# Two graph-attention layers: a block's leftovers held behind a step, and moved weight tiles summed in SBUF

## The chip, the cores and the metric

One NeuronCore of a Trainium2 chip runs the whole program. The metric is the device time of one execution in microseconds (us). Engines are named as in the profile: PE is TensorE (PEld its weight loads), DVE is VectorE, ACT is ScalarE, POOL is GpSimd, SP is SyncE, which here only issues transfers.

## The reference

4096 nodes with 512 features and a 4096 x 4096 adjacency `adj` pass through two layers. All data are float32. Cut to what matters:

```python
# layer 0, h = relu(layernorm(x)); 4 heads of 128
sig = sigmoid(f1[:, :, None] + f2[:, None, :])
att = softmax(where(adj != 0, adj * sig, -inf))     # both patterns are adj
Xa  = einsum('hij,hjd->hid', att, Xw)               # encoder attention
emb = mlp_block(batchnorm(Xa))
Y   = einsum('hij,hjd->hid', att, emb)              # decoder attention, the same att
out = mlp_block(elu(Y @ W.T));  x = x + out
# layer 1, h = relu(layernorm(x)); 4 heads of 128
logits = leaky_relu(e_s[:, :, None] + e_n[:, None, :]) - 1e10 * (1 - adj)
x = x + relu(einsum('hnm,hmo->hno', softmax(logits), feats) + b)
```

So there are three attentions: encoder, decoder (it uses the encoder's weights and denominators again) and the last one, in the second layer.

## The kernel before

Features lie on the partitions, nodes along the free dimension. One function, `attention`, is used three times. It works in 8 blocks, one for each head h and each half tb of the target nodes (TB = 2048). A block walks over NJ = 32 steps j of 128 source nodes. In a step

- SP loads a 256 KB mask tile `a` (5 buffers);
- the weights of 128 sources by 2048 targets are made in a 1 MB tile `e`: in encoder and decoder by Tanh (L402) and Exp (L403) on ACT and the multiplication by the mask on DVE (L404); in the last attention by one ACT operation (L771) and one on DVE (L772);
- PE multiplies the tile into four PSUM banks `po` (L334; the fourth bank is opened in step EVICT = 2, and catches up with L331).

The tiles `e` come from a ring: two buffers in a pool that lives through layer 0 and `ebufs` in the attention's own pool, so 9 in the encoder and in the last attention, and 6 in the decoder. A tile that nobody has finished with holds up ACT's first operation nine steps later.

The softmax's denominator is a sum over all sources. Each step's tile goes into it in one of three ways, which a table of steps lays down (`ENC_FIRST` for the encoder's first two blocks, `ENC` for its others, `GAT` for the last attention):

- *by ones*: PE multiplies the tile by a column of ones into the bank `den` (L288);
- *added*: DVE adds the tile to an SBUF tile `acc` (L352, L354; in the last attention it is a part of R[2]);
- *moved*: a GpSimd-issued DMA adds the tile to the DRAM tile `dacc[tb]` (L346; a block's first move is a plain copy). In step NJ - 2 the sum is loaded back into a tile of the ring (L304).

At the end of a block PE multiplies the loaded sum and `acc` by ones as well. `ENC_FIRST` has no moved steps and 12 by ones; `ENC` has 9 moved and 6 by ones; `GAT` has 11 moved and 3 by ones.

What remains of a block, its *leftovers*, is done in the course of the next block. The function `at(j, f)` files it under a step, and the loop calls it at the beginning of that step: in step 2 the denominators are copied out (L235 on ACT) and sent through DRAM into a column (L236 and L238 on GpSimd's queue), and the four banks are evicted (L496 on DVE in the encoder, L607 or L776 on ACT in the others); in step 7 the column is inverted (L242, L243) and stored as a row (L244); in steps 8, 9, 14 and 15 each of four pieces of that row is broadcast to a tile `rb` (L249, 2 buffers); in steps 13, 14, 19 and 20 the results are scaled by it (L500, or L780 in the last attention), and one step later they are finished (L503 statistics in the encoder; L613 to L615 in the decoder; L783 and an addition to the output in DRAM, L789, in the last attention). The decoder has no L242, as it takes the encoder's rows.

In the encoder every fifth tile is also stored in DRAM for the decoder (L321, L372 on ACT's queue).

The order in which a step's instructions are traced is not the order of an engine's queue. A scheduler that knows only modelled durations lays out each engine's queue ahead of time: of the instructions that it takes to be ready, it issues the one traced first. An instruction whose operands it takes to be ready early can so come before work of earlier steps. `tc.issue_after(ins)` forbids this for one place: instructions traced inside it that run on the engine of `ins` come behind `ins` in that engine's queue, without a wait. On the chip each queue is worked off in order.

Of the kernel before, what the change touches and what calls it, by code (L numbers as in the profile page):

```python
# [20 lines left out]

# [1 line left out]

# [6 lines left out]
FP = mybir.dt.float32  # L32
U8 = mybir.dt.uint8
AF = mybir.ActivationFunctionType
ALU = mybir.AluOpType
# [4 lines left out]
N, F, H, D, P = 4096, 512, 4, 128, 128  # L40
IB = 512
NIB = N // IB
NJ = N // P
C = IB // P

TB = 2048
NTB = N // TB
SB = TB // IB
# [8 lines left out]
TINY = 1e-30  # L57
# [4 lines left out]
ENC_FIRST = (), (4, 5, 10, 11, 15, 16, 20, 21, 25, 26, 30, 31)  # L62
ENC = (0, 3, 6, 9, 12, 15, 18, 21, 24), (4, 5, 13, 14, 30, 31)
GAT = (0, 2, 5, 7, 10, 12, 15, 17, 20, 22, 25), (9, 30, 31)
# [15 lines left out]
def kernel(ctx, tc, x, xT, adjT, w0, w0T, v0, wencT, wdecT, vecs, w1, w1T, a1, outT):  # L80
    nc = tc.nc
    consts = ctx.enter_context(tc.tile_pool(name="consts", bufs=1))
    dram = ctx.enter_context(tc.tile_pool(name="dram", bufs=1, space=DRAM))
# [5 lines left out]
    R = [big.tile([P, N], FP, name=f"R{i}") for i in range(5)]  # L89
# [30 lines left out]
    jcol = consts.tile([P, NTB, H, NJ // NTB], FP, name="jcol")  # L120
    jcol2 = consts.tile([P, NTB, H, NJ // NTB], FP, name="jcol2")
    nq = consts.tile([P, NTB, H, NJ // NTB], FP, name="nq")

    def column(t, j, h):
        j = j % (NJ // NTB), j // (NJ // NTB)
        return t[:, j[1], h, j[0]:j[0] + 1]
# [19 lines left out]
    ekeep = [[[dram.tile([P, TB], FP, name=f"ekeep{h}_{t}_{k}") for k in range(NJ // KEEP)] for t in range(NTB)]  # L146
             for h in range(H)]

    dacc = [dram.tile([P, TB], FP, name=f"dacc{n}") for n in range(2)]

    masks = [[dram.tile([MG * P, TB], U8, name=f"mask{t}_{g}") for g in range(NJ // MG)] for t in range(NTB)]

# [43 lines left out]
    def load_mask(a, tb, j):  # L196

        return nc.sync.dma_start(a, masks[tb][j // MG][(j % MG) * P:(j % MG + 1) * P, :])


    def attention(what, keep, pools, weights, values, row_of, out, finish, ebufs, modes=None, invert=None,
                  kept=None, sums=None, extras={}, row0=None, masks0=()):

# [15 lines left out]
        spool, made, masks0 = pools, 0, list(masks0)  # L221
        if invert is not None:
            acc = spool.tile([P, TB], FP, name="acc") if sums is None else sums

        def weight_tile():
            nonlocal made
# [45 lines left out]
            load_row(rowb, *row_of(h, tb))  # L272
            return rowb

        later, last_ones, last_main = {}, None, None
        rowb = row0 if row0 is not None else next_row_of(0, 0)
        blocks = [(h, tb) for h in range(H) for tb in range(NTB)]
        for n, (h, tb) in enumerate(blocks):
# [6 lines left out]
            def add_to_den(t, stop=False):  # L285
                nonlocal begun, last_ones
                for s in range(SB):
                    last_ones = nc.tensor.matmul(den[s * 32:(s + 1) * 32, :], ones[:, 0:32], t[:, s * IB:(s + 1) * IB],  # L288
                                                 start=not begun, stop=stop)
                begun = True  # L290
# [1 line left out]
            po, ahead = [bank() for _ in range(SB - 1)], []  # L292
            adds, held, back, stores, next_row = [], [], None, [], None
            for j in range(NJ):
                for f in later.pop(j, []):
                    f()
                with tc.issue_after(a_load.ins) if j else nullcontext():
                    if (n, j) in extras:
                        extras[n, j](a_load)
                    if not last and j == NJ - 10:  # L300
                        next_row = next_row_of(*blocks[n + 1])
                if moved and j == NJ - 2:
                    back = weight_tile()
                    nc.gpsimd.dma_start(back, dacc[tb])  # L304
                e = weight_tile()
                store = j % KEEP == KEEP - 1 and kept is not None
                if store and kept == "read":
                    a_load = nc.sync.dma_start(e, ekeep[h][tb][j // KEEP])
                else:
                    if masks0:  # L310
                        a, a_load = masks0.pop(0)
                    else:
                        a = mask_tile(keep)
                        a_load = load_mask(a, tb, j)
                    weights(e, rowb, a, j, h, SB if n + j == 0 else 1)
                    if store:
                        stores.append((j // KEEP, e))

                    if j % KEEP == KEEP - 3 and stores:
                        k, t = stores.pop()  # L320
                        nc.scalar.dma_start(ekeep[h][tb][k], t)  # L321

                def products():
                    nonlocal last_main, last_ones

                    with tc.issue_after(last_ones.ins) if last_ones is not None else nullcontext():

                        if j == EVICT:
                            po.append(bank())
                            for k, t in ahead:  # L330
                                nc.tensor.matmul(po[-1], block(values[h], k), t[:, (SB - 1) * IB:SB * IB],  # L331
                                                 start=(k == 0), stop=False)
                        for s, b in enumerate(po):
                            last_main = nc.tensor.matmul(b, block(values[h], j), e[:, s * IB:(s + 1) * IB],  # L334
                                                         start=(j == 0), stop=(j == NJ - 1))
                    last_ones = None


                early = last and j == NJ - 1 and invert is not None
                if not early:  # L340
                    products()
                if j < EVICT:
                    ahead.append((j, e))
                if invert is not None:
                    if j in moved:
                        nc.gpsimd.dma_start(dacc[tb], e, **({"accum_op": ALU.add} if j > moved[0] else {}))  # L346
                    elif j in by_ones:
                        held.append(e)
                    else:
                        adds.append(e)  # L350
                        if len(adds) == 2:
                            nc.vector.tensor_add(acc, *adds)  # L352
                        elif len(adds) > 2:
                            nc.vector.tensor_add(acc, acc, e)  # L354

                    if held and j + 1 not in by_ones:
                        with tc.issue_after(last_main.ins):
                            for t in held:
                                add_to_den(t)
                        held = []  # L360
                    if j == NJ - 1:
                        with tc.issue_after(last_ones.ins) if last_ones is not None else nullcontext():
                            if back is not None:
                                add_to_den(back)
                            add_to_den(acc, True)
                if early:
                    products()
# [32 lines left out]
    def tanh_weights(e, rowb, a, j, h, parts):  # L400
        for e, rowb, a in in_parts(parts, e, rowb, a):
            nc.scalar.activation(e, rowb, AF.Tanh, bias=column(score[:, 1], j, h), scale=0.5)  # L402
            nc.scalar.activation(e, e, AF.Exp, scale=0.5)  # L403
            nc.vector.tensor_mul(e, e, a)  # L404

    a_att, b_att, a_mlp, b_mlp = (coefs[:, k, :] for k in range(4))

    with tc.tile_pool(name="keep", bufs=1) as keep:
# [116 lines left out]
        with tc.tile_pool(name="enc", bufs=1) as spool:  # L525

            with tc.issue_after(last_act.ins), tc.issue_after(masks0[-1][1].ins):
                attention("enc", keep, spool, tanh_weights, R[0:4], lambda h, tb: (rows[tb], h), out_enc,
                          (scaled, statistics), 7, lambda n: ENC if n > 1 else ENC_FIRST, (TINY, ALU.max), "write",
                          row0=row0, masks0=masks0,  # L530
                          extras={(1, 12): lambda load: copy_adjacency(7, load),
                                  (2, 8): encoder_weights, (H * NTB - 1, NJ // 2): three_heads})
# [232 lines left out]
    def gat_weights(e, rowb, a, j, h, parts):  # L765
        for e, rowb, a in in_parts(parts, e, rowb, a):

            if parts > 1:
                nc.vector.tensor_scalar(rowb, rowb, mbc[:, h:h + 1], G_MAX, ALU.add, ALU.min)
                nc.scalar.activation(rowb, rowb, AF.Exp, scale=0.8)  # L770
            nc.scalar.activation(e, rowb, AF.Relu, bias=column(nq, j, h), scale=column(jcol, j, h))  # L771
            nc.vector.scalar_tensor_tensor(e, e, column(jcol2, j, h), a, ALU.add, ALU.mult)  # L772

    def out_gat(spool, h, tb, s, po):
        o = R[2][:, TB + s * IB:TB + (s + 1) * IB]
# [15 lines left out]
    with tc.tile_pool(name="gat", bufs=1) as spool:  # L791
        x1_last = []

        def load_last(load):
            x1_last.append(spool.tile([P, TB], FP, name="rowb", bufs=2))
            nc.sync.dma_start(x1_last[0], outT[(H - 1) * P:H * P, (NTB - 1) * TB:NTB * TB])

        attention("gat", spool, spool, gat_weights, v1, lambda h, tb: (rowsg, tb * H + h), out_gat,
                  (scaled_gat, add_to_output), 7, lambda n: GAT, (N * TINY, ALU.add), sums=R[2][:, 0:TB], row0=row0,
                  extras={(H * NTB - 1, NJ - 10): load_last})  # L800


# [40 lines left out]
```

## Time and profile before

| | us |
|---|---|
| median of 3 runs | 3362.6 (3361.0 to 3365.4) |
| the profiled execution: its own time | 3363.46 |
| its span, from first to last instruction | 3361.7 |
| encoder attention, first to last product | 69.7 to 1115.1 |
| decoder attention | 1261.3 to 2150.3 |
| last attention | 2414.8 to 3351.2 |
| PE busy | 3246.9 |
| DVE busy | 2680.3 |
| ACT busy | 2601.9 |

The mean granted TensorE clock was 0.987. In the profile, an instruction's line is followed by its operation and by out<-in in the program's names of tiles. "Idle before" is the time that the engine stood still just ahead of it, and "<-" names what ended that. The windows view gives the busy time of each engine in a stretch and the number of instructions begun there in brackets. A queue with a q behind the engine's name is that engine's sequencer, which issues transfers. One matmul of 512 float32 columns shows as two instructions, 0.43 us apart, so a step has 8 in the row L334; four products by ones run side by side in the array, so their rows overlap.

### The profile page before, as it was taken

To read this page: it belongs to the slowest core of one execution; us is meant where nothing else is said; L and a number is where in the kernel's file an instruction comes from. 1 tells how busy PE (TensorE), PEld (TensorE's weight loads), DVE (VectorE), ACT (ScalarE), POOL (GpSimd) and SP (SyncE) were. 2 spreads that over 40 slices of the span, in tenths; PEclk is the share of its full clock that TensorE was granted. 3 is DMA by queue.
4 is the path that set the end of the run, shared out by engine and by line. 5 is a ranking of instruction groups with operands and counts; after the bars stand their busy time and mean duration, and the time that the engine had idled before them with its cause. 6 is when DMAs were issued, how large, how long until landed. Compare 5 with 4: busy or idle time off the path is not lost. (4 is left out here: it accounts for less than half of the span.)

```text
span 3361.7 us, 26034 instructions
## 1 busy us (share of the span) xinstructions
PE 3246.9 (97%) x8943; PEld 1495.3 (44%) x8943; DVE 2680.3 (80%) x1912; ACT 2601.9 (77%) x1908; POOL 327.4 (10%) x479
## 2 busy tenths in 40 slices
PE   7999999999999999999999999999999999999999
PEld 6334334334334464444444444447644444443443
DVE  6999889889888775665666566486599999989999
ACT  7989999999999438999999999566655665665654
POOL 2000110110110000000000000024301111111111
PEclk9999999999999999999999999999999999999999
DMA  9985768768777103443443443232288898788877
GB/s 204 195 178 166 213 195 235 216 196 233 213 212 199 43 13 138 138 135 128 147 151 124 138 145 130 75 113 95 69 205 204 203 229 207 196 198 207 212 191 173
DMA packets 180309, 559.60 MB, mean 166 GB/s; under 512 B 20372, under 2 KB 23700, under 8 KB 144208
## 3 DMA queue, kind: packets, MB, share of 16 engines
q0 software_dynamic: 43232, 211.14, 31.8%
q1 hardware_dynamic: 126288, 293.66, 25.6%
q10 hardware_dynamic: 10656, 53.15, 4.0%
q8 instruction: 70, 1.15, 0.1%
q14 instruction: 63, 0.52, 0.0%
HBM read 391.78 MB, written 233.19 MB: 186 GB/s over the span
## 5 line engine op out<-in xcount | busy, mean ns | idle before, releaser
L334 PE MATMUL ps<-e,R 128*128 128x512 f32 x6048 | 2651.6, 598 | 77.4 <-DVE e L404 60.4
L334 PEld LDWEIGHTS ps<-e,R 128*128 128x128 f32 x6048 | 1149.2, 191 | 1570.6 <-issue 1420.9
L404 DVE TENSOR_TENSOR e<-e,a 128x2048 f32<-128x2048 f32 (+1 forms) x470 | 1050.6, 2260 | 385.6 <-ACT e L403 363.7
L402 ACT ACTIVATE e<-rowb,score 128x2048 f32<-128x2048 f32 (+1 forms) x470 | 913.3, 1968 | 85.0 <-PE ps L334 47.4
L403 ACT ACTIVATE e<-e 128x2048 f32<-128x2048 f32 (+1 forms) x470 | 872.3, 1881 | 29.9 <-DVE e L404 23.5
L771 ACT ACTIVATE e<-rowb,nq,jcol 128x2048 f32<-128x2048 f32 x224 | 457.9, 2087 | 208.6 <-DMA dacc<-e 132.3
L772 DVE SCALAR_TENSOR_TENSOR e<-e,jcol,a 128x2048 f32<-128x2048 f32 (+1 forms) x259 | 590.6, 2319 | 3.8 <-ACT e L771 3.8
L354 DVE TENSOR_TENSOR R<-R,e 128x2048 f32<-128x2048 f32 x128 | 292.0, 2282 | 0.0
L354 DVE TENSOR_TENSOR acc<-acc,e 128x2048 f32<-128x2048 f32 x126 | 288.3, 2288 | 2.3
L346 POOL DMA_DIRECT2D dacc<-e x142 | 118.5, 835 | 1213.8 <-DMA dacc<-e 413.7
L543 PE MATMUL ps<-R,w 128*128 128x512 f32 x512 | 220.3, 592 | 0.6 <-DVE w L510 0.6
L249 POOL DMA_DIRECT2D rb<-rinvs x88 | 52.8, 652 | 1118.6 <-DVE R L500 903.9
L543 PEld LDWEIGHTS ps<-R,w 128*128 128x128 f32 x512 | 97.2, 190 | 122.7 <-issue 118.2
L717 PE MATMUL ps<-w1x,hT 128*128 128x260 f32 x512 | 117.8, 389 | 2.8 <-ACT hT L693 2.8
L563 ACT ACTIVATE ex<-ps,bias 128x512 f32<-128x512 f32 x64 | 44.0, 687 | 97.2 <-PE ps L543 80.1
L783 ACT ACTIVATE R<-R,vec 128x512 f32<-128x512 f32 x32 | 23.0, 720 | 110.4 <-DVE R L780 110.1
L717 PEld LDWEIGHTS ps<-w1x,hT 128*128 128x128 f32 x512 | 97.9, 193 | 22.8 <-ACT hT L693 4.4
L500 DVE TENSOR_TENSOR R<-R,rb 128x512 f32<-128x512 f32 x60 | 40.5, 685 | 70.7 <-DMA rb<-rinvs 58.6
L288 PE MATMUL den<-e,ones 128*32 128x512 f32 x784 | 93.6, 598 | 0.0
L771 ACT ACTIVATE e<-w,nq,jcol 128x2048 f32<-128x2048 f32 (+1 forms) x35 | 65.6, 1939 | 32.9 <-DMA dacc<-e 30.2
L565 DVE SCALAR_TENSOR_TENSOR ex<-ex,re 128x512 f32<-128x512 f32 x64 | 45.0, 703 | 35.8 <-ACT re L564 35.7
L722 ACT ACTIVATE R<-ps,rstd 128x128 f32<-128x128 f32 x128 | 38.7, 367 | 40.2 <-PE ps L717 39.2
(154 smaller groups left out, 1217.0 us busy)
## 6 DMA issues: line engine op xcount, KB each, us to landing
a<-mask SPq DMA_DIRECT2D x720, 256.0 KB, 3.6
dacc<-e POOLq DMA_DIRECT2D x142, 1024.0 KB, 8.6
ekeep<-e ACTq DMA_DIRECT2D x48, 1024.0 KB, 5.7
e<-ekeep SPq DMA_DIRECT2D x48, 1024.0 KB, 4.8
rb<-rinvs POOLq DMA_DIRECT2D x88, 256.0 KB, 3.8
mask<-in_adjT POOLq DMA_DIRECT2D x8, 2048.0 KB, 76.6
rowb<-rows SPq DMA_DIRECT2D x16, 1024.0 KB, 5.2
e<-dacc POOLq DMA_DIRECT2D x14, 1024.0 KB, 5.1
```

The lines of the kernel that those rows point to most:

```text
L249: nc.gpsimd.dma_start(rb, everywhere(rinvs[h][tb], 0, s * IB, IB))
L288: last_ones = nc.tensor.matmul(den[s * 32:(s + 1) * 32, :], ones[:, 0:32], t[:, s * IB:(s + 1) * IB], start=not begun, stop=stop)
L334: last_main = nc.tensor.matmul(b, block(values[h], j), e[:, s * IB:(s + 1) * IB], start=(j == 0), stop=(j == NJ - 1))
L346: nc.gpsimd.dma_start(dacc[tb], e, **({"accum_op": ALU.add} if j > moved[0] else {}))
L354: nc.vector.tensor_add(acc, acc, e)
L402: nc.scalar.activation(e, rowb, AF.Tanh, bias=column(score[:, 1], j, h), scale=0.5)
L403: nc.scalar.activation(e, e, AF.Exp, scale=0.5)
L404: nc.vector.tensor_mul(e, e, a)
L543: nc.tensor.matmul(z, w[:, fb, o * P:(o + 1) * P], nodes(src[fb], ib), start=(fb == 0), stop=(fb == C - 1))
L717: nc.tensor.matmul(b[:, 0:2 * DX], hT[:, fb, c * P:(c + 1) * P], w1x[:, fb, 2 * k:2 * k + 2, :].rearrange("p h x -> p (h x)"), start=(fb = ...
L771: nc.scalar.activation(e, rowb, AF.Relu, bias=column(nq, j, h), scale=column(jcol, j, h))
L772: nc.vector.scalar_tensor_tensor(e, e, column(jcol2, j, h), a, ALU.add, ALU.mult)
```

## The change

Two things are changed together.

*Pins.* The functions that make weights now return their last ACT and their last DVE instruction. The leftovers filed under a step j are traced inside `pinned(products_of)`, that is, behind these two instructions of the last step whose weights were computed. Transfers that GpSimd or SP issue and PE's instructions are not held by it.

*The moved tiles' sum.* From an attention's second block on, moved tiles are added to a tile in SBUF, `sums2`, and PE takes it from there; nothing is loaded back. Only a first block with moved steps (the last attention's) still goes by DRAM, through one tile `dacc` in place of two. In the encoder the tile is new (`acc2`, 8 KB in each partition), and `ebufs` goes from 7 to 6, so that its ring has 8 tiles. In the last attention it is `row0`, the tile that held the first block's row (in memory, the decoder's weights `w`), and the ring stays at 9. There is one `sums2` for all blocks, where `dacc` had one tile for each half.

```diff
-    dacc = [dram.tile([P, TB], FP, name=f"dacc{n}") for n in range(2)]
+    dacc = dram.tile([P, TB], FP, name="dacc")
...
+    @contextmanager
+    def pinned(behind):
+
+        with ExitStack() as stack:
+            for i in behind:
+                stack.enter_context(tc.issue_after(i.ins))
+            yield
...
+            sums2 = spool.tile([P, TB], FP, name="acc2") if sums2 is None else sums2
...
-                for f in later.pop(j, []):
-                    f()
+
+                with pinned(products_of):
+                    for f in later.pop(j, []):
+                        f()
...
-                if moved and j == NJ - 2:
+                if n == 0 and moved and j == NJ - 2:
                     back = weight_tile()
-                    nc.gpsimd.dma_start(back, dacc[tb])
+                    nc.gpsimd.dma_start(back, dacc)
...
-                    weights(e, rowb, a, j, h, SB if n + j == 0 else 1)
+                    products_of = weights(e, rowb, a, j, h, SB if n + j == 0 else 1)
...
-                        nc.gpsimd.dma_start(dacc[tb], e, **({"accum_op": ALU.add} if j > moved[0] else {}))
+                        nc.gpsimd.dma_start(sums2 if n else dacc, e, **({"accum_op": ALU.add} if j > moved[0] else {}))
...
-                            if back is not None:
-                                add_to_den(back)
+                            if moved:
+                                add_to_den(sums2 if n else back)
                             add_to_den(acc, True)
...
-            nc.scalar.activation(e, e, AF.Exp, scale=0.5)
-            nc.vector.tensor_mul(e, e, a)
+            last_act = nc.scalar.activation(e, e, AF.Exp, scale=0.5)
+            last_dve = nc.vector.tensor_mul(e, e, a)
+        return last_act, last_dve
...
-                          (scaled, statistics), 7, lambda n: ENC if n > 1 else ENC_FIRST, (TINY, ALU.max), "write",
+                          (scaled, statistics), 6, lambda n: ENC if n > 1 else ENC_FIRST, (TINY, ALU.max), "write",
...
-            nc.scalar.activation(e, rowb, AF.Relu, bias=column(nq, j, h), scale=column(jcol, j, h))
-            nc.vector.scalar_tensor_tensor(e, e, column(jcol2, j, h), a, ALU.add, ALU.mult)
+            last_act = nc.scalar.activation(e, rowb, AF.Relu, bias=column(nq, j, h), scale=column(jcol, j, h))
+            last_dve = nc.vector.scalar_tensor_tensor(e, e, column(jcol2, j, h), a, ALU.add, ALU.mult)
+        return last_act, last_dve
...
-                  (scaled_gat, add_to_output), 7, lambda n: GAT, (N * TINY, ALU.add), sums=R[2][:, 0:TB], row0=row0,
+                  (scaled_gat, add_to_output), 7, lambda n: GAT, (N * TINY, ALU.add), sums=R[2][:, 0:TB],
+                  sums2=row0, row0=row0,
```

More of the change, by code (lines that the diff above doesn't have):

```diff
@@ L24 @@
-from contextlib import ExitStack, nullcontext
+from contextlib import ExitStack, contextmanager, nullcontext
 import concourse.bass as bass
@@ L198, in load_mask @@
         return nc.sync.dma_start(a, masks[tb][j // MG][(j % MG) * P:(j % MG + 1) * P, :])
+    @contextmanager
[4 more added lines that the diff above has]
+            yield
     def attention(what, keep, pools, weights, values, row_of, out, finish, ebufs, modes=None, invert=None,
-                  kept=None, sums=None, extras={}, row0=None, masks0=()):
+                  kept=None, sums=None, sums2=None, extras={}, row0=None, masks0=()):
         spool, made, masks0 = pools, 0, list(masks0)
@@ L273, in next_row_of @@
             return rowb
-        later, last_ones, last_main = {}, None, None
+        later, last_ones, last_main, products_of = {}, None, None, ()
         rowb = row0 if row0 is not None else next_row_of(0, 0)
```

## The prediction

> **What bounds the kernel now.** I read the page first, then busy time in windows cut at the blocks, then the waits, and then the order of one engine's queue at the start of a block. The page's first line says that TensorE is busy nearly all the time, so anything that shortens another engine counts only where TensorE waits for it:
>
> ```profile
> PE 3246.9 (97%) x8943; PEld 1495.3 (44%) x8943; DVE 2680.3 (80%) x1912; ACT 2601.9 (77%) x1908; POOL 327.4 (10%) x479
> ```
>
> A busy matmul row is no proof of full pace, so I cut the three attentions into their eight blocks each (from the first matmul of a block to the next one's):
>
> ```profile
> core 0: us, PE busy (x) PEld busy (x) DVE busy (x) ACT busy (x) POOL busy (x), PEclk, DMA share, GB/s
> ...
> 595.20:722.20 127.00, 120.25 (x324) 50.44 (x320) 114.78 (x63) 119.21 (x65) 11.89 (x17) 0.99 0.76 215
> ...
> 1381.10:1491.00 109.90, 109.90 (x258) 48.67 (x257) 65.98 (x39) 102.95 (x61) 2.15 (x4) 1.00 0.41 138
> ...
> 2762.50:2877.30 114.80, 114.80 (x301) 49.54 (x297) 110.38 (x55) 70.96 (x42) 16.40 (x22) 1.00 0.83 208
> 2877.30:2994.80 117.50, 115.77 (x300) 49.22 (x296) 111.80 (x56) 70.96 (x42) 17.21 (x23) 1.00 0.83 205
> 2994.80:3116.10 121.30, 116.52 (x300) 48.98 (x296) 112.50 (x56) 70.55 (x42) 17.25 (x23) 1.00 0.82 199
> ```
>
> Decoder blocks (1381 on) take 109.9 us with TensorE busy for 109.90: nothing is to be had there. The last attention's block 3 runs at 114.8, all TensorE; blocks 4 to 7 take 117.5, 121.3, 117.7 and 117.4. An encoder block (block 4, at 595) takes 127.0 with TensorE 120.25, ScalarE 119.21, VectorE 114.78: three engines near their limit and none full, the mark of engines stalling one another. The waits name the stalls:
>
> ```profile
> DVE R L500 <- DMA rb<-rinvs: 58.6, 19, 7.9
> ACT dsb L235 <- PE den L288: 45.4, 7, 11.2
> PE ps L334 <- DVE e L404: 60.4, 35, 5.2
> DVE dcol L242 <- DMA dcol<-dens: 30.8, 7, 8.8
> ```
>
> And the timeline of VectorE at the start of encoder block 4 shows where the first of them lies:
>
> ```profile
> 586.58 4.49 DVE L404 TENSOR_TENSOR e<-e,a 128x2048 f32<-128x2048 f32 x2
> ...
> 597.72 4.49 DVE L404 TENSOR_TENSOR e<-e,a 128x2048 f32<-128x2048 f32 x2 [4.25 <-ACT e L403]
> ...
> 605.10 4.49 DVE L404 TENSOR_TENSOR e<-e,a 128x2048 f32<-128x2048 f32 x2 [0.31 <-ACT e L403]
> 616.85 0.69 DVE L500 TENSOR_TENSOR R<-R,rb 128x512 f32<-128x512 f32 x1 [7.26 <-DMA rb<-rinvs]
> ```
>
> Count the masks' multiplications L404: steps 0 to 5, and then the scaling L500 of the block before, which the program traces in step 13. The scheduler has put it seven steps early, where its row of reciprocals has not landed, and all of VectorE stands behind it for 7.26 us. In the last attention the timelines of GpSimd and VectorE show the other one, at block 7:
>
> ```profile
> 3244.47 0.86 POOL L346 DMA_DIRECT2D dacc<-e  x1 [8.69 <-issue]
> 3245.03 0.86 POOL L236 DMA_DIRECT2D dens<-dsb  x1
> 3252.79 0.59 POOL L238 DMA_DIRECT2D dcol<-dens  x1 [6.89 <-DMA dens<-dsb]
> ...
> 3254.66 0.17 DVE L242 TENSOR_SCALAR dcol<-dcol 128x16 f32<-128x16 f32 x1 [5.66 <-DMA dcol<-dens]
> ```
>
> The denominators were in SBUF by 3235.9 (their copy is ScalarE's L235), but their 8 KB transfer stands in GpSimd's queue behind the third moved tile of the block, which waits for the landing of the second (3243.68), and then it lands with that tile.
>
> **The change, part by part.** (1) *Pins.* No instruction is added. Leftovers of a block on ScalarE and VectorE may no longer come before the weights of step j-1. I compared queue positions: eviction L496 and copy L235 already stand behind step 1 in the encoder, as traced in step 2, so the 45.4 us wait of L235 is not touched; in the last attention L776, L780 and L242 stand at or behind their traced steps too, so there the pins are void. In the decoder L500 and L613 to L615 move about ten steps later; about 10 of L500's 58.6 us lie there and cost nothing, since TensorE covers them (109.90 of 109.9); without that cover it would be those 10. What moves in the encoder is L242 (from behind step 3 to 6), L500 and L503 (from behind 5 to 7 to behind 12 to 20).
>
> The rb chain gets time: L242 behind step 6 runs near 615; rinvs behind a moved tile took 5.7 us in this block, so near 621 to 625; rb took 5.7 us, 631 to 635; step 12 ends on VectorE near 638. So the 7.3 us wait goes (48 us in the encoder). What is late next? From ScalarE's restart after L235 (595.9) its Exp rows L403 come in pairs every 7.39 us, so that of step 16 ends at 649.4. VectorE, no longer late, idles before step 16 and starts it at 649.4; before, it started it at 653.3. From there to the end of step 30's multiplication it was busy without a gap, 58.2 us (to 711.5); the second half of the leftovers, 4 rows of 0.6 to 0.7, now falls into this stretch: 60.7. Then 10.9 us to the end of the denominator on TensorE, as before. A block from restart to restart: 0.6 + 53.5 + 60.7 + 10.9 = 125.7. So of 7.3 us only about 1.4 come back: VectorE's own work in the second half (five additions in a row in steps 25 to 29) and ScalarE's wait for the denominator keep the rest. Against 130.4, 126.7, 127.1, 127.3, 126.9 for blocks 2 to 6 (between L235 rows) this is 4.7 + 1.0 + 1.4 + 1.6 + 1.2 = 9.9. Block 1 differs: from 260 on TensorE has no gap, and its 6 us of gaps (steps 3 to 10) come just from VectorE being late by the leftovers; later these meet a lead, so I take 5 of the 6. Block 7 gets 1.5 as its neighbours do; its wait for the bias product, 7.8 us at L517, isn't pinned and stays. Encoder: 16.4.
>
> (2) *Moved tiles into SBUF.* 142 moves before and after (6 x 9 and 8 x 11), issued on the same queue; 13 of 14 loads back (L304; 0.56 us of queue, 5.1 to landing) go, and in the last attention the e buffer that each took. Each chain stays serial, as each addition waits for the one before. The trace has no addition into SBUF. Nearest rows: an addition in DRAM lands after 8.6 us (8.2 in the last attention), a plain 1 MB transfer after 5.1. The Trainium skill's page "DMA: Bandwidth & Descriptors" speaks against the change: by "Anatomy of one DMA — SWDGE (gpsimd) path" and the SBUF-side ceiling under "Specifications", a transfer costs 2.0 us plus its bytes at some 436 GB/s; two reads and a write of 1 MB, all now on SBUF's side, make an estimate of 9.2. In the last attention, 5.1 + 10 x (8.2 + 0.5) = 92 us of 114.8 by the row, 5.1 + 10 x 9.7 = 102 by the rule: hidden both ways. I take 8.2, with 5.1 and 9.2 as ends.
>
> (3) *A new wait.* dacc alternated between two tiles; the SBUF sum is one, so a block's first move waits until TensorE has read the last block's sum, just ahead of the denominator's end. It delays that move by 2 us in block 7 (3229.1 to about 3231), more where VectorE leads more. Behind it in GpSimd's queue stands just the dens transfer, which needs the same end of the denominator. For the moves this makes them later than dens in their readiness: after the first move (a copy, 5.1 us) the next is ready 5.6 us after the denominator's end, dens about 4.6 (3235.9 against 3231.3). So I expect dens ahead of the second or third move; it then lands by about 6 to 14 us after the denominator, dcol 2 us later, and L242 comes up some 17 us after it (3248.9): its waits of 4.4 to 8.8 us go. Blocks 4 to 7 then run at TensorE's 114.8: 2.7 + 6.5 + 2.9 + 2.6 = 14.7; I count 14.5, leaving a little for a dens that still lands late.
>
> (4) *Encoder ring from 9 to 8 e tiles.* A moved tile is held about 7.4 (Tanh to Exp), 4 to 6 (VectorE), 9 (landing): 21 to 25 us; a stored one 14.8 to its issue and 6 to 8 more; ring 8 gives 8 x 3.69 = 29.5. I cost it at nothing; the cover is 4 us, and one landing of 13 us (there is one of 12.9 in block 4) uses it up.
>
> Sum: 16.4 + 14.5 = 30.9. The profiled execution took 3363.46 (span 3361.7), 0.9 above the median of 3362.6; 3363.5 - 30.9 = 3332.6, on the median's scale 3331.7; I say 3331.
>
> **The rivals.** *ScalarE becomes the encoder's bound.* If the new order also puts the multiplications of steps 30 and 31 ahead of waiting additions, L235 no longer waits and a block takes ScalarE's 119: 11.4 + 7.7 + 8.1 + 8.3 + 7.9 in blocks 2 to 6, about 8 each in 1 and 7, 59 in all; with the last attention 74, so 3289. For it: ScalarE's 119.21 is the largest sum that nothing moves. Against: nothing in the change orders additions. Halfway there gives 3310.
>
> *The last attention keeps its wait.* If GpSimd's order stays (first three moves, then dens), everything shifts by the new wait of 2 us, the wait at L242 grows from 5.7 to 7.7, and about 1.5 us is lost in blocks 3 to 7: +7.5. With the encoder's 16.4: 3354. For it: L242 waits over 4 us in five of seven blocks now.
>
> *The ring of 8 stalls ScalarE.* One wait of 2 to 3 us in each of 6 blocks undoes most of the encoder's gain: about 3346.
>
> *Slower: additions in SBUF are slow.* The 11 moves of a last-attention block must land inside it: 5.1 + 10 x (L + 0.5) = 114.8 gives L = 10.5. Beyond it the chain sets the block. At L = 12: 130 against 114.8, 15 us in each of 7 blocks, 106 less the encoder's 16: about 3450. For it: DMA share is 0.83 there already, and single landings reach 12.9. Against: two streams into the same engines made 8.2 out of 5.1, and the rule gives 9.2.
>
> That the change doesn't do what it says is part of the first step: pins in the last attention and on L235 are void.
>
> **How the numbers follow.** Main line 0.57 (own range 3318 to 3344); ScalarE bound or halfway 0.14 (3285 to 3315); last attention keeps its wait 0.15 (3344 to 3358); ring 0.07 (3340 to 3362); slow additions 0.05; other delays of order 0.02. The range 3302 to 3354 leaves out half of the second and the edges of the rest, about 0.2. A difference under 0.2% (7 us) can't be told from none: slower over 3369 takes 0.07 (slow additions and the 0.02), same 0.03 (ends of ring and order), faster 0.90.
>
> **What would show it.** After: L500 in the encoder behind step 12 or later with a wait sum of about 10 (decoder's) instead of 58.6; L235's waits about as before; encoder blocks 2 to 6 near 125.7; L242's waits under 5 in sum, and last blocks at 114.8; moves landing after 7 to 9 us. Wrong it would be by encoder blocks near 119 or 127, by a landing above 10.5, by ScalarE waiting at L402 for moved tiles in the encoder, or by L242 still waiting.

## The result, and the profile after

The changed kernel takes 3346.4 us (median of four runs, 3344.5 to 3349.1) against 3364.0 for the kernel before in runs on the same chips (3361.0 to 3366.4): 17.6 us less, a ratio of 0.9949 with a 95% interval of 0.9931 to 0.9966. The forecast was 3331, in a range of 3302 to 3354. So the direction holds and the range holds the time, but of the 31 us forecast a little over half came, and the main line's own range (3318 to 3344) is missed by 2 us.

The profiled execution of after took 3349.09 (span 3347.3); against the profiled 3363.46 (span 3361.7) that is 14.4 less. It is the highest of its four runs, which is why two profiles differ by 3 us less than the medians do. Where the 14.4 lies, from windows cut at the first matmul of each block:

| us | before | after | forecast | found |
|---|---|---|---|---|
| encoder, block 0 | 138.8 | 139.7 | 0 | +0.9 |
| encoder, block 1 | 129.5 | 137.8 | -5 | +8.3 |
| encoder, blocks 2 to 6 | 638.4 | 623.5 | -9.9 | -14.9 |
| encoder, block 7 | 138.8 | 132.6 | -1.5 | -6.2 |
| last attention, all blocks | 936.4 | 934.3 | -14.5 | -2.1 |

These make 14.0 of the 14.4; the rest is spread outside these blocks. The decoder's blocks stay at 109.9. (In after the weights' multiplication L404 is L417, the scaling L500 is L514 and in the last attention L795, the denominator's copy L235 is L246, dcol's use L242 is L253, and rb's load L249 is L260.) On the page the engines' busy times hardly move: VectorE's 2680.3 us are 2679.2, TensorE's 3246.9 are 3239.2, with as many instructions (8943) and a mean granted clock of 0.990 for 0.987. So the change moves waits, not work; no run tells what the clock's 0.003 is worth by itself. The windows show where: encoder block 1 (at 210) and block 4 (at 598), and the last attention's block 5. The first number behind the window is its length, then each engine's busy time. Block 1 before comes first:

```profile
core 0: us, PE busy (x) PEld busy (x) DVE busy (x) ACT busy (x) POOL busy (x), PEclk, DMA share, GB/s
208.50:338.00 129.50, 124.06 (x364) 50.56 (x360) 122.00 (x67) 119.32 (x65) 5.22 (x9) 1.00 0.60 163
```
```profile
210.20:348.00 137.80, 127.31 (x364) 51.46 (x360) 121.86 (x67) 119.32 (x65) 5.19 (x9) 0.96 0.54 150
...
598.40:722.70 124.30, 119.04 (x324) 49.66 (x320) 114.45 (x63) 119.22 (x65) 11.55 (x17) 1.00 0.75 212
...
2982.70:3101.90 119.20, 116.10 (x301) 49.19 (x297) 112.54 (x56) 70.67 (x42) 16.66 (x23) 1.00 0.80 194
```

An encoder block is still bound by no one engine (124.3 against ScalarE's 119.22), and the last attention still has blocks above 114.8. The waits name what is left (sum, number, longest):

```profile
ACT dsb L246 <- PE den L299: 44.9, 7, 11.2
...
DVE R L795 <- DMA rb<-rinvs: 29.5, 6, 6.7
DVE R L514 <- DMA rb<-rinvs: 13.0, 3, 11.9
```

The scaling's 58.6 us are down to 13.0, of which one wait, in encoder block 1, makes 11.9, and VectorE no longer waits for dcol (30.8 before). The last attention has a new one of nearly the same size in its place: the scaling L795 on rb, 29.5. The copy's wait for the denominator is as it was, 45.4 before and 44.9 now.

VectorE's timeline in encoder block 4 shows the edit at work. The scaling now runs behind step 12 without a wait:

```profile
639.48 2.29 DVE L417 TENSOR_TENSOR e<-e,a 128x2048 f32<-128x2048 f32 x1
641.68 0.68 DVE L514 TENSOR_TENSOR R<-R,rb 128x512 f32<-128x512 f32 x1
...
649.14 4.49 DVE L417 TENSOR_TENSOR e<-e,a 128x2048 f32<-128x2048 f32 x2 [0.58 <-ACT e L416]
...
709.75 8.89 DVE L417 TENSOR_TENSOR e<-e,a 128x2048 f32<-128x2048 f32 x4
```

Where block 1 loses is read off GpSimd's and VectorE's timelines. GpSimd's queue issues the 2 MB adjacency cast (L446) that this block's last eight steps are the first to read, and right behind it two rb loads. After comes first, then the same queue before:

```profile
233.50 0.78 POOL L446 DMA_DIRECT2D mask<-in_adjT  x1
234.97 1.08 POOL L260 DMA_DIRECT2D rb<-rinvs  x2 [0.69 <-DMA rinvs<-dcol]
```
```profile
219.62 1.07 POOL L249 DMA_DIRECT2D rb<-rinvs  x2 [1.45 <-DMA rinvs<-dcol]
...
233.22 0.78 POOL L432 DMA_DIRECT2D mask<-in_adjT  x1 [6.66 <-DMA a<-mask]
```

VectorE in after:

```profile
264.53 0.69 DVE L514 TENSOR_TENSOR R<-R,rb 128x512 f32<-128x512 f32 x1 [11.86 <-DMA rb<-rinvs]
```

In the trace the cast landed at 263.86 and rb at 264.51, 29.5 us after its issue. Before, all four rb loads had been issued from 219 to 226, ahead of the cast, and landed within 5 us.

The last attention's DMA issues tell its story in three rows. The last column is the median us from issue to landing; before stands first, after second.

```profile
dens<-dsb POOLq DMA_DIRECT2D x7, 8.0 KB, 7.6
dcol<-dens POOLq DMA_DIRECT2D x7, 8.0 KB, 1.9
rinvs<-dcol POOLq DMA_DIRECT2D x7, 8.0 KB, 2.2
```
```profile
dens<-dsb POOLq DMA_DIRECT2D x7, 8.0 KB, 3.6
dcol<-dens POOLq DMA_DIRECT2D x7, 8.0 KB, 8.2
rinvs<-dcol POOLq DMA_DIRECT2D x7, 8.0 KB, 7.5
```

dens came free of the moves, as forecast, and dcol and rinvs were caught by them instead: 7.6 + 1.9 + 2.2 = 11.7 us in the three small transfers before, 3.6 + 8.2 + 7.5 = 19.3 after.

### The profile page after: what moved, and what is told of

Read it like the earlier page. It is cut to its first block, busy times and chain, and to the rows that moved or that the text cites. A ratio compares the mean times of both kernels' runs of the same rounds, so it can differ in the third digit from the quotient of the medians.

```text
span 3347.3 us, 26017 instructions
## 1 busy us (share of the span) xinstructions
PE 3239.2 (97%) x8943; PEld 1490.7 (45%) x8943; DVE 2679.2 (80%) x1912; ACT 2599.7 (78%) x1908; POOL 321.9 (10%) x466
## 3 DMA queue, kind: packets, MB, share of 16 engines
q0 software_dynamic: 41360, 197.51, 30.7%
## 4 chain that ended last, share of the span: by engine, by line
PE 46%; DVE 24%; issue 12%; ACT 9%; DMA 8%; DVEq 0%; ACTq 0%; POOL 0%; POOLq 0%
PE ps L347 31%; DVE e L786 8%; PE ps L557 7%; DVE e L417 6%; DVE R L367 6%; ACT e L415 5%; PE ps L731 3%; DMA w<-e 3%; ACT e L416 3%; DVE acc L367 2%; DMA rb<-rinvs 2%; DMA a<-mask 2%; PE den L299 1%; PE ps L490 1%; PE ps L612 1%
## 5 line engine op out<-in xcount | busy, mean ns | idle before, releaser
L417 DVE TENSOR_TENSOR e<-e,a 128x2048 f32<-128x2048 f32 (+1 forms) x470 | 1052.6, 2260 | 426.0 <-ACT e L416 404.1
L260 POOL DMA_DIRECT2D rb<-rinvs x88 | 54.6, 652 | 1135.2 <-DVE R L514 834.5
L359 POOL DMA_DIRECT2D w<-e x77 | 64.9, 843 | 620.7 <-DVE e L786 255.5
L359 POOL DMA_DIRECT2D acc<-e x54 | 45.7, 846 | 635.5 <-DVE e L417 340.0
L299 PE MATMUL den<-e,ones 128*32 128x512 f32 x680 | 82.5, 599 | 0.0
L579 DVE SCALAR_TENSOR_TENSOR ex<-ex,re 128x512 f32<-128x512 f32 x64 | 44.9, 701 | 35.7 <-ACT re L578 35.7
```

What stands on the lines that cost most here:

```text
L260: nc.gpsimd.dma_start(rb, everywhere(rinvs[h][tb], 0, s * IB, IB))
L359: nc.gpsimd.dma_start(sums2 if n else dacc, e, **({"accum_op": ALU.add} if j > moved[0] else {}))
L417: last_dve = nc.vector.tensor_mul(e, e, a)
```

## The experiments

Each kernel is compared with the kernel before on the same chip. Two questions were open: which part gave the 17.6 us, and where the missing 13 went.

**The pins alone.** The sum goes back to DRAM, the ring to nine tiles.

```diff
-    dacc = dram.tile([P, TB], FP, name="dacc")
+    dacc = [dram.tile([P, TB], FP, name=f"dacc{n}") for n in range(2)]
...
-                        nc.gpsimd.dma_start(sums2 if n else dacc, e, **({"accum_op": ALU.add} if j > moved[0] else {}))
+                        nc.gpsimd.dma_start(dacc[tb], e, **({"accum_op": ALU.add} if j > moved[0] else {}))
...
-                          (scaled, statistics), 6, lambda n: ENC if n > 1 else ENC_FIRST, (TINY, ALU.max), "write",
+                          (scaled, statistics), 7, lambda n: ENC if n > 1 else ENC_FIRST, (TINY, ALU.max), "write",
```

> Pins alone: the moved tiles go to DRAM and come back as before, ring of 9 in the encoder. My theory (the two parts act in different places): the encoder is as in the changed kernel, blocks 2 to 6 near 124.3 us, block 7 near 132.6, and block 1 near 138 with the 12 us wait at the first scaling L514 behind the adjacency cast; the last attention as before (waits at L253 of about 30 us in sum, blocks 4 to 7 at 117.5 to 121). In all 12 us under the kernel before. Rival (the sum in SBUF and the ring of 8 matter in the encoder too): blocks 2 to 6 differ from 124.3 by over 1 us, and the total by over 5 us from -12.

Measured: 3349.5 (3349.2 to 3350.0), ratio 0.9947 (0.9932 to 0.9962). Encoder block 4 is after's, the last attention's block 5 is before's:

```profile
598.10:722.40 124.30, 119.02 (x325) 49.70 (x321) 114.48 (x63) 119.22 (x65) 12.07 (x17) 1.00 0.79 220
...
2982.10:3103.80 121.70, 116.66 (x301) 48.99 (x297) 112.50 (x56) 70.59 (x42) 17.14 (x23) 1.00 0.83 199
```

All that the encoder gains, and what its block 1 loses (138.3 here), comes from the pins. With nine tiles blocks 2 to 6 take 126.3, 124.1, 124.3, 124.1 and 124.6; with eight 126.4, 124.0, 124.3, 124.1 and 124.7: the ring of eight costs nothing. By the ratios the pins alone give all that the change gives (0.9947 against 0.9949). The 2.1 us that the last attention gains in after are no more than this stage differs by among kernels that share its code: it takes 934.3 in after, 937.1 and 939.1 in two kernels below that change only the encoder.

**The SBUF sum alone.**

```diff
-                with pinned(products_of):
+                with nullcontext():
```

> The SBUF sum and the ring of 8 alone, without pins. My theory: the encoder is as before (block 1 129.5, blocks 2 to 6 at 127 to 130, waits at the scaling of 7.3 us a block), the last attention as in the changed kernel (the column's wait gone, scaling waits of about 29 us in sum), in all 2 us under the kernel before. Rival (the ring of 8 costs time that the pins hid): encoder blocks longer than before by over 1 us each.

Measured: 3357.9 (3355.2 to 3360.6), ratio 0.9974 (0.9962 to 0.9987). Encoder block 4 is back at

```profile
595.10:721.90 126.80, 121.40 (x324) 51.14 (x320) 114.78 (x63) 119.21 (x65) 11.36 (x17) 0.97 0.75 207
```

with the unpinned scaling waiting (44.1 us at L514 in the encoder). The last attention has the new wait without any pin: 30.7 us at L795. So moving the sum traded the dcol wait for the rb wait by itself. The ratio gives this kernel more than expected; its profile is 5.5 us shorter, in pieces of about a microsecond (encoder 1.3, the decoder's first block 1.3, last attention 1) that I could not trace to one cause. The two gains (18 and 9 us by the ratios) also add up to more than the whole change brings; the intervals of the ratios are 8 to 10 us wide.

**Fewer additions late in an encoder block.** The forecast's reason for the small return was VectorE's full stretch from step 16 on. Two of the tiles that TensorE sums by a column of ones were moved from the block's start into that stretch, so that VectorE adds less there.

```diff
-ENC = (0, 3, 6, 9, 12, 15, 18, 21, 24), (4, 5, 13, 14, 30, 31)
+ENC = (0, 3, 6, 9, 12, 15, 18, 21, 24), (13, 14, 27, 28, 30, 31)
```

> The changed kernel, with the encoder's steps by ones at (13, 14, 27, 28, 30, 31) in place of (4, 5, 13, 14, 30, 31): as many products and additions, but two additions of 2.2 us move from the end of a block to its beginning, where VectorE has idle time. My theory (VectorE's own work from step 16 on sets the end of a block, ScalarE then waits 4.7 us for the denominator): blocks 2 to 6 fall from 124.3 to about 120, the wait at the copy of the denominators from 4.7 to under 1, in all about 22 us under the changed kernel. Rival (ScalarE's pace and the small waits set the block): no change within 1 us a block.

Measured: 3341.4, ratio 0.9922 (0.9907 to 0.9936); blocks 3 to 6 take 123.0 to 123.6, not 120: about 1 us of the expected 4. VectorE's lag is gone: in block 4 its multiplication of step 30 starts 0.3 us behind the end of ScalarE's Exp, 4.8 in after. TensorE's timeline at the end of block 4 shows why:

```profile
694.27 7.13 PE L347 MATMUL ps<-e,R 128*128 128x512 f32 x16 [1.54 <-DVE e L417]
...
703.19 10.57 PE L347 MATMUL ps<-e,R 128*128 128x512 f32 x24
713.68 1.92 PE L299 MATMUL den<-e,ones 128*32 128x512 f32 x16
715.42 1.90 PE L299 MATMUL den<-acc,ones 128*32 128x512 f32 x16
```

TensorE starts behind VectorE (1.54 us of wait) and then runs without a gap to the end of the denominator: the products by ones, 1.9 us for each two tiles, are now its own tail.

**The four small transfers on SyncE's queue.** If the moves and the cast hold rb back, it comes free on a queue without them. (SyncE's queue carries the mask tiles, 256 KB each.)

```diff
-            nc.gpsimd.dma_start(dens[h][tb], dsb[0:P:32, :])
+            nc.sync.dma_start(dens[h][tb], dsb[0:P:32, :])
...
```

(and the same for the loads of dcol, rinvs and rb)

> The changed kernel, with the leftovers' four small transfers (dens, dcol, rinvs, rb) on SP's queue instead of GpSimd's. My theory (each lands with the megabytes that stand ahead of it in GpSimd's queue): the wait of 11.9 us at the first scaling of encoder block 1 goes (block 1 from 138 to about 128), the scaling waits in the last attention (29 us in sum) go, its blocks 3 to 7 run at 114.8 (from 115.4, 116.9, 119.2, 118.8, 116.2: 12 us), in all 20 us under the changed kernel. Rival (the transfers are slow since all DMA engines are full): rb still lands after 8 us and more beside the moves, and both waits stay; or SP, waiting for them, holds up mask tiles, and new waits for masks appear.

Measured: 3324.9 (3323.3 to 3325.1), ratio 0.9873 (0.9858 to 0.9887), 21.5 under after. Encoder block 1 and the last attention's block 5:

```profile
206.60:336.00 129.40, 124.85 (x365) 50.39 (x361) 122.05 (x67) 119.33 (x65) 1.32 (x2) 1.00 0.61 164
...
2966.30:3081.20 114.90, 114.90 (x301) 49.64 (x297) 112.79 (x57) 71.02 (x42) 12.72 (x16) 1.00 0.84 202
```

Block 1 gives back its 8.4 us, and all last-attention blocks from 1 to 6 run at TensorE's pace of 114.8. The order of this chain in block 5, on SyncE's queue here and on GpSimd's in after:

```profile
2973.85 0.32 SPq L249 DMA_DIRECT2D dcol<-dens  x1
...
2984.69 0.32 SPq L255 DMA_DIRECT2D rinvs<-dcol  x1
...
2988.47 0.80 SPq L260 DMA_DIRECT2D rb<-rinvs  x2
```
```profile
2988.43 0.91 POOL L359 DMA_DIRECT2D w<-e  x1 [2.76 <-DMA w<-e]
2989.02 0.89 POOL L249 DMA_DIRECT2D dcol<-dens  x1
...
3006.53 0.86 POOL L359 DMA_DIRECT2D w<-e  x1 [8.12 <-DMA w<-e]
3007.49 0.57 POOL L255 DMA_DIRECT2D rinvs<-dcol  x1
...
3016.08 0.85 POOL L359 DMA_DIRECT2D w<-e  x1 [8.02 <-DMA w<-e]
3016.64 1.44 POOL L260 DMA_DIRECT2D rb<-rinvs  x2
```

In after every step of the chain from dcol on is issued within 1 us behind a 1 MB move (`w<-e`), which has itself waited for the landing of the last one. From dcol's issue to rb's it takes 27.6 us; on SyncE's queue 14.6.

The gain is not that a small transfer lands free of the moves there. In this block a move is in flight from 2971.68 to 2979.66 (by the trace's landings), dcol is issued into it at 2973.85, and VectorE gets it just behind the move's landing:

```profile
2979.84 0.18 DVE L253 TENSOR_SCALAR dcol<-dcol 128x16 f32<-128x16 f32 x1 [2.11 <-DMA dcol<-dens]
```

All 14 waits for dcol in this kernel and in the next two end 0.2 to 0.4 us behind the landing of a move that was issued ahead of dcol. So the rival named in the expectation is right in part. What the other queue saves is the place in line: a link is issued when its operands are there, and not behind the next move. VectorE's waits for dcol come back with 8.9 us in sum and its waits for mask tiles at L417 rise from 11.1 to 15.4, at no cost to these blocks.

In encoder block 1 the cast is still there, in flight from 229.59 to 260.99. GpSimd, SyncE's queue and VectorE:

```profile
229.59 0.75 POOL L446 DMA_DIRECT2D mask<-in_adjT  x1 [175.45 <-DMA a<-mask]
```
```profile
230.57 0.80 SPq L260 DMA_DIRECT2D rb<-rinvs  x2
```
```profile
252.51 0.69 DVE L514 TENSOR_TENSOR R<-R,rb 128x512 f32<-128x512 f32 x1
```

The scaling runs without a wait 8.5 us before the cast lands. So the cast's traffic alone does not hold rb until then; the wait came with rb's place behind the cast in GpSimd's queue.

**What the SBUF sum is worth once the small transfers are off the queue.** The same four edits, with the sum in DRAM as in the kernel with the pins alone.

> Pins and small transfers on SP's queue, but the moved tiles' sum in DRAM as before (e5 without the second part of the change). My theory (the SBUF sum gained only by the order that it gave to GpSimd's queue; a move lands after 8.1 us in SBUF and 8.2 in DRAM): as e5 within 4 us, encoder blocks 124.3, last attention at 114.8. Rival (the SBUF sum is worth something by itself, as the 8 us of e2 suggest): 6 to 10 us over e5.

Measured: 3327.0 (3324.3 to 3328.0), ratio 0.9884 (0.9868 to 0.9901). The intervals of this and of the kernel with the SBUF sum (3324.9) overlap, and their encoders and last attentions agree within 0.4 us: once the small transfers are off the queue, the sum's place makes no difference that this measurement can tell.

**The kernel before with its small transfers on SyncE's queue.** It asks whether the encoder's wait, too, was only the queue.

> The kernel before, with only the four small transfers moved to SP's queue; no pins, the moved tiles' sum in DRAM. My theory (the wait at the scaling is the chain dens, dcol, rinvs, rb, of which only rinvs and rb stood behind moves there): the early scaling after step 5 still comes before its row, by 2 to 4 us in place of 7.3; encoder blocks 124 to 126, the column's wait in the last attention goes (12 us), in all 25 us under the kernel before. Rival (the order alone makes the wait, queues do not matter): 7 us stays in the encoder.

Measured: 3346.3, ratio 0.9945 (0.9928 to 0.9961): these four moved transfers alone bring as much as the whole change. The last attention's blocks are at 114.8 to 115.3, though L242 still waits 17.6 us for dcol in sum (4.3 at most). The encoder's wait stays, as the rival had it. VectorE first, then SyncE's queue, in block 4:

```profile
618.17 0.69 DVE L500 TENSOR_TENSOR R<-R,rb 128x512 f32<-128x512 f32 x1 [7.55 <-DMA rb<-rinvs]
```
```profile
605.85 0.32 SPq L244 DMA_DIRECT2D rinvs<-dcol  x1
612.48 1.59 SPq L249 DMA_DIRECT2D rb<-rinvs  x2
```

From rinvs to rb it takes 6.6 us even off GpSimd's queue: a move is in flight from 603.55 to 612.25, and rb is issued 0.2 us behind its landing. In the encoder it is the order on VectorE that makes the wait, and of the kernels run only those with pins lose it; in the last attention it is GpSimd's queue, and the pins do nothing there.

**The cast earlier in block 1.** It is traced in step 8 instead of 12, so that it might land before the scaling.

```diff
-                          extras={(1, 12): lambda load: copy_adjacency(7, load),
+                          extras={(1, 8): lambda load: copy_adjacency(7, load),
```

> The changed kernel, with the last adjacency cast (2 MB) of encoder block 1 traced in step 8 and not in step 12, so that it stands ahead of rinvs in GpSimd's queue and not between rinvs and rb. My theory (rb waits in the queue for the cast's landing, 30 us after its issue): the cast lands some 12 to 15 us earlier, rinvs with it, and the wait of 11.9 us at the first scaling falls to 0 to 4 us; block 1 from 138 to about 130. Rival (the copies' traffic slows rb wherever it stands): the wait stays near 12.

Measured in one run: 3343.3. GpSimd, then VectorE:

```profile
217.92 0.77 POOL L446 DMA_DIRECT2D mask<-in_adjT  x1 [3.06 <-DMA a<-mask]
...
251.85 1.09 POOL L260 DMA_DIRECT2D rb<-rinvs  x2 [20.44 <-DMA rinvs<-dcol]
```
```profile
255.64 0.69 DVE L514 TENSOR_TENSOR R<-R,rb 128x512 f32<-128x512 f32 x1 [5.07 <-DMA rb<-rinvs]
```

The cast is 15.6 us earlier. Now rinvs is caught (20.7 us from issue to landing), rb is not (3.8), and the wait falls from 11.9 to 5.1, the block from 137.8 to 131.1. The wait follows the cast, as it should if the cast is its cause.

**What holds an encoder block at 124.** With the small transfers on SyncE's queue, three kernels try the two remaining suspects: two of VectorE's additions taken out of the middle (their tiles are summed by ones, and two at the block's start are added for them); the denominator's copy traced two steps later on ScalarE, when TensorE is done with it; and both.

```diff
-ENC = (0, 3, 6, 9, 12, 15, 18, 21, 24), (4, 5, 13, 14, 30, 31)
+ENC = (0, 3, 6, 9, 12, 15, 18, 21, 24), (13, 14, 19, 20, 30, 31)
```

> Small transfers on SP's queue as in e5, and the encoder's steps by ones at (13, 14, 19, 20, 30, 31) in place of (4, 5, 13, 14, 30, 31). In e4 the two steps taken from the end added 1.7 us of products by ones to TensorE's last steps; here they are taken from the middle, where the leftovers L514 and L517 lie. My theory (VectorE's work between step 16 and the end sets the block): 4.4 us less of it, blocks 2 to 6 near 120.5, in all about 20 us under e5. Rival (ScalarE's pace from its restart after the denominator to step 31, and what TensorE does after it, set the block): 123 to 124, under 6 us in all.

Measured: 3315.6, ratio 0.9855 (0.9840 to 0.9869); blocks 3 to 6 take 123.3, about 1 us less, and block 7 takes 128.2 for 132.4. VectorE now waits for ScalarE until step 25 (675.14), and then falls behind again:

```profile
675.14 4.49 DVE L417 TENSOR_TENSOR e<-e,a 128x2048 f32<-128x2048 f32 x2 [0.70 <-ACT e L416]
...
697.53 8.89 DVE L417 TENSOR_TENSOR e<-e,a 128x2048 f32<-128x2048 f32 x4
```

Its multiplication of step 30 (697.53) starts 3.8 us behind the end of ScalarE's Exp, 4.8 in after. So steps 16 to 24 hardly count: the additions of steps 25 to 29 make most of the lag.

```diff
-            dcol = denominators(h, tb, den) if den is not None else None
...
-            if dcol is not None:
-                at(EVICT + 5, invert_them, h, tb, dcol)
+            if den is not None:
+                def copied():
+                    at(EVICT + 5, invert_them, h, tb, denominators(h, tb, den))
+                at(EVICT + 2, copied)
```

> As e5, but the denominators are copied out in step 4 and not in step 2 (evictions stay in step 2), so ScalarE reaches the copy two steps, 7.4 us, later than now. My theory (ScalarE's wait for the denominator, 4.7 us a block, keeps the gain small): the wait at the copy goes, blocks 2 to 6 fall from 124.3 to 119 to 121, in all 25 us under e5. Rival (the wait is only slack, and VectorE's work sets the block): the wait goes, and ScalarE waits instead for tiles of the ring, blocks at 123 to 124.

Measured: 3306.2 (3306.0 to 3306.4), ratio 0.9827 (0.9812 to 0.9841), 18.6 under the kernel with the small transfers moved (that one ran on another chip; by the ratios it is 15). Blocks 2 to 6 take 120.5 to 121.1. And with both edits:

> f1 and f2 together. If VectorE's work and ScalarE's wait each hold part of it, this is the fastest, blocks 2 to 6 at ScalarE's own 119 and 30 us under e5; if one of them alone holds all of it, this equals the better of f1 and f2 within 5 us.

Measured: 3294.6 (3292.7 to 3295.3), ratio 0.9791 (0.9777 to 0.9806), the fastest here. The copy's wait in encoder block 4, in after and with both edits:

```profile
ACT dsb L246 <- PE den L299: 4.7, 1, 4.7
```
```profile
ACT dsb L246 <- PE den L300: 0.4, 1, 0.4
```

The window of block 4 with both:

```profile
576.10:695.80 119.70, 118.00 (x325) 50.07 (x321) 114.59 (x64) 119.21 (x65) 7.46 (x10) 1.00 0.78 220
```

At 119.7 against ScalarE's 119.21 the block is ScalarE's. The block's length follows the copy's wait: in after, with the additions moved, with the copy late and with both, waits of 4.7, 4.0, 1.1 and 0.4 us go with blocks of 124.3, 123.3, 120.7 and 119.7. So most of an encoder block's missing 5 us was one in-order wait, ScalarE standing at the start of each block for TensorE's last product. VectorE's additions of steps 25 to 29 help to make that product late; tracing the copy later lets ScalarE go on meanwhile.

## Why the forecast was right in direction and half in size

That the time fell into the range is in part luck. Block 1 missed its term by 13.3 us and the last attention by 12.4; the encoder's other blocks from 2 on brought 9.7 more than forecast.

- *The pins take the scaling behind step 12, and its wait goes* (step 1): shown. It runs at 641.7 without a wait, and the pins alone make the whole encoder difference. The copy L246 keeps its 45 us, as the forecast said. The decoder's 9.5 us of waits at the scaling, which the forecast expected to stay, fell to 1.1, at no gain: its blocks are at 109.9 before and after.
- *Of 7.3 us about 1.4 come back, as VectorE's stretch and the copy's wait keep the rest*: between copies block 4 takes 124.3, forecast 125.7. From step 15 (649.14) to the end of step 30's multiplication the trace has 62.9 us; from step 16, where the forecast's stretch begins, a step (2.2) less, 60.7: exact. Mis-sized is the term 53.5, as step 16 begins 1.3 us sooner after ScalarE's restart than reckoned; over blocks 2 to 6 it is 14.9 in place of 9.9. The two reasons given for the small return are links of one chain, and the runs weigh them. Of VectorE's stretch, steps 16 to 24 give 1 us; the five additions in a row, which the forecast named, do make VectorE late, but taking two of them out (0.3 us of lag left) gave only 1 us as well, as their products fell into TensorE's tail. The copy's place gives 3.6, with the additions of the middle moved 4.6, to ScalarE's bound.
- *Block 1 gains 5*: it lost 8.3, and the failed step is a landing. rb's 5.7 us were taken from block 4; in block 1 a 2 MB cast stands ahead of it in GpSimd's queue when the pins hold the chain back, and rb needs 29.5. The working looked at VectorE's order and not at what the later chain would meet in GpSimd's. The kernel with the cast moved (wait 5.1 for 11.9) and the one with the transfers moved (no wait) both show it.
- *Block 7 gains 1.5*: 6.2. The pins give it (132.4 with them alone, 138.0 with the sum alone). The wait for the bias product, which the forecast left at 7.8, is 2.6 in after, with 3.3 us of waiting for ScalarE just ahead of it. Which order makes this no run isolates.
- *Moves into SBUF land after 8.2 us, ends 5.1 and 9.2*: right, and the row beats the rule. The page has

```profile
w<-e POOLq DMA_DIRECT2D x77, 1024.0 KB, 8.1
```

  for the last attention, where additions in DRAM took 8.2; the estimate of 9.2 that was worked out from the Trainium skill's "DMA: Bandwidth & Descriptors" ("Anatomy of one DMA — SWDGE (gpsimd) path") is too high for it. No slow addition, so no part of the slower rival.
- *dens goes ahead of a move, dcol lands 2 us later, L242's waits go, 14.5 us come*: the first and third are right, the second is the step that failed, and with it the last. dcol's 1.9 us was a row in which no move stood just ahead of it. In after, in block 5, dcol goes behind the second move and takes 8.4, rinvs behind the fourth (8.5) and rb behind the fifth (8.3). The working followed the first of four transfers of one queue and stopped at the wait it wanted gone; rb's wait took its place, at 29.5 us for 30.8:

```profile
3024.97 0.69 DVE L795 TENSOR_TENSOR R<-R,rb 128x512 f32<-128x512 f32 x1 [6.66 <-DMA rb<-rinvs]
```

- *The ring of eight costs nothing*: shown, by the kernel with nine.
- *The rivals.* By time alone the result lies where "the last attention keeps its wait" was put (3344 to 3358), and its substance, that a wait of this size stays there, is true; its mechanism is not, as GpSimd's order did change. "ScalarE becomes the bound" did not happen, but it named the copy's wait as what stands between 124 and ScalarE's 119, and the kernel with both edits is there, by another way than the order that this rival supposed. The stalled ring and the slow additions did not come.

Open stay block 7's gain and the microseconds by which the sum alone beats what its stages show.

## What to carry to other kernels

When a wait is to go, follow every link of the chain behind it through the queue that issues it, and ask for each what large transfer is issued just ahead at its new time; a small transfer's median is worth nothing once the order has changed. A chain of small transfers belongs on a queue in which it need not stand behind large ones that wait for each other; it may still land only with a large one in flight. Reordering an engine belongs to the places where the engine's order, and not a queue, makes the wait. And where three engines are near their limit, look first for an instruction that one of them waits for at the block's start: tracing that copy two steps later brought about as much here as the whole change, once the queue was clear.

## What the hardware showed that was not expected

- In the last attention an 8 KB transfer issued just behind a 1 MB addition lands with it: dcol took 1.8 to 2.0 us before, issued ahead of the next move, and 7.7 to 9.2 in six of the seven blocks after, issued behind one. dens went the other way, from a median of 7.6 to 3.6, when its place in the queue changed.
- SyncE's queue does not change that: 14 of 14 waits for dcol ended 0.2 to 0.4 us behind a move's landing, and rinvs, issued into a move in encoder block 4, took 6.6 us to rb's issue. Why a transfer of one queue lands only with the move of another, no run shows.
- Behind a 2 MB cast of the same queue a 256 KB load took 29.5 us. Issued on SyncE's queue 1 us behind the cast, it was in use after 22 us, with the cast still in flight.
- Adding 1 MB to a tile in SBUF takes as long as adding it in DRAM: 8.1 against 8.2 us in the last attention, 8.5 against 9.0 in the encoder.
